# Feature sums, numerators and second pieces of the first fourth-layer batches: from VectorE to GpSimd

## The chip, the cores and the metric

The kernel runs on one core of a Trainium2 chip. The metric is the device time of one execution in microseconds (us); lower is better. A core has five engines with instruction queues of their own: TensorE (PE, with weight loads shown apart as PEld), VectorE (DVE), ScalarE (ACT), GpSimd (POOL) and SyncE (SP), which here only issues DMAs. Each queue runs strictly in its order, and engines wait for each other through semaphores.

## The reference

Four graph layers on x of 8 batches x 2048 nodes x 64 features, with one adjacency matrix of 2048 x 2048 for all batches. After each layer x becomes layernorm(x + layer(x)). The first three layers are attention layers; the fourth weighs each feature by itself:

```python
def _L2_gnn_ref(x, adj, W, a):
    h = jnp.matmul(x, W)
    ...
    e = jax.nn.leaky_relu(f1[:, :, None] + f2[:, None, :], negative_slope=ALPHA)
    e = jnp.where(adj[None, :, :] > 0, e, NEG_BIG)
    attention = jax.nn.softmax(e, axis=2)
    h_prime = jnp.matmul(attention, h)
    return jax.nn.relu(h_prime)

def _L3_gnn_ref(x, w0, b0, wa, ba, adj):
    feat = jax.nn.softplus(x * (INV_SQRT2 * w0[0, 0]) + b0[0])
    scores = feat * wa + ba
    mask = adj > 0
    logits = scores[:, None, :, :] * mask[None, :, :, None].astype(scores.dtype)
    logits = jnp.where(mask[None, :, :, None], logits, jnp.float32(-1000000000.0))
    attn = jax.nn.softmax(logits, axis=2)
    out = jnp.einsum('bijd,bjd->bid', attn, feat)
    return out
```

In the fourth layer the scores depend on the source node and the feature alone. So its softmax is a quotient of two products with the mask: the numerator is mask x (feat * exp(scores)), the denominator is mask x exp(scores). A node without any edge gets the mean of feat over all nodes instead, for which the kernel needs the sum of feat.

## The kernel before

**Units and steps.** Layers 1 to 3 are cut into 24 units, one for each layer and batch. Units 0 to 15 are the first two layers, units 16 to 23 the third layer, so unit 16 + b is batch b's third layer. In the code `now[1]` is the running unit's number. A unit has 16 steps, one for each block of 128 source nodes. In a step of the third layer VectorE makes the weights w of 128 x 2048 out of a row r in PSUM and the mask `edge` in SBUF (`weights`), ScalarE takes their exponential (`exponential`), and PE adds their product to the sums `acc` (`products`). VectorE may run two steps ahead (`reach`), and w has four buffers, so weights of a step wait until PE has used those of four steps before. The row r is one single tile: the next unit's row is spread over it by PE (`spread`) when VectorE has made its last weights of a unit.

**Ends of units.** When a unit's products are done, a generator is put into the background streams (`bg`); each step of the main loop moves every stream on to its next `yield`, which interleaves the unit's end with the steps of the next unit. For the third layer that is first `finish`: copy acc, transpose it on PE (p_o), divide on VectorE (den, o), layernorm. Then comes `l3_features`, which the diff touches. Because the finish takes most of a unit, the softplus of batch b falls at the end of unit 17 + b and what follows it at the start of unit 18 + b. All instructions of PE, VectorE, ScalarE and GpSimd keep the order in which the program emits them; only DMAs are ordered by the framework.

**What `l3_features` does for a batch.** It stores x (tile x_d), computes softplus on ScalarE and one addition on VectorE into f (in place of x, so the profile names it x), then on GpSimd d = f * wa + l3off. The sum of f over a partition's 16 nodes goes to fs, which PE sums over the partitions (p_fm) and VectorE turns into the mean fm (`l3_mean`). ScalarE takes exp(d), VectorE makes the numerator f * d. Then each of the two, f and d, is split into two pieces: ScalarE rounds it [...] (`q.v[0]`), and the rest `q.v[1]` is what a subtraction leaves; four subtractions of 128 x 512 for a batch. Two batches make a pair (i is 0 for the even batch, 1 for the odd one). In the version before, the even batch's subtractions are on GpSimd, the odd one's on VectorE.

**Layer 4's products.** When both batches of a pair are ready, `l3_products` multiplies the pieces with mask blocks (p_l, 32 matmuls for a block of 128 nodes), half a block between two steps of the units from 19 on. Their place in PE's queue is fixed when the program is built. The mask comes in quarters by DMA from a copy in memory (mask_d). `l3_finish` divides on VectorE (nd), adds the mean term, normalizes and stores.

**Group 1.** At the same time, at the turn from unit 17 to unit 18, the generator `group` prepares the constants of the batches 4 to 7: a handful of VectorE operations of 128 x 64 (s_g, tt_g, lo_g, down_g), one exponential on ScalarE (te), then 256 small matmuls (p_lse_g) spread over the steps of unit 18, and again small VectorE operations (am_g, tt_g).

All instructions of the four compute engines are recorded by one helper at line 80, so the profile names them by their tiles.

Of the kernel before, what the change touches and what calls it, by code (L numbers as in the profile page):

```python
# [8 lines left out]
F32 = mybir.dt.float32  # L9
# [6 lines left out]
ALU = mybir.AluOpType  # L16
AX = mybir.AxisListType

P = 128
# [31 lines left out]
def gnn4_kernel(ctx: ExitStack, tc: tile.TileContext, t, out):  # L51
    nc = tc.nc
    x_in, adjT = t["x"], t["adjT"]
    B, N, F = x_in.shape
# [9 lines left out]
    small = ctx.enter_context(tc.tile_pool(name="small", bufs=2))  # L64
# [42 lines left out]
    class Banks:  # L107
# [4 lines left out]
        pool = None  # L112
# [28 lines left out]
    pe, dve, act, pool = (InOrder(e) for e in (nc.tensor, nc.vector, nc.scalar, nc.gpsimd))  # L141

    def psum(name):
        return pm.tile([P, 512], F32, tag="pm", name=name)
# [4 lines left out]
    def bc_k(v, n=K, f=F):  # L149
        return v[:, None, :].to_broadcast([P, n, f])  # L150
# [65 lines left out]
    src = t["L0_gnn_a"]  # L216
# [6 lines left out]
    p = psum("p_nodes")  # L223
# [157 lines left out]
    def softplus(f, y, src, layer=2):  # L381

        act.activation(y, src, AF.Abs, scale=l3c[:, 0:1], bias=l3c[:, 1:2])
        act.activation(y, y, AF.Exp, scale=-1.0)
        yield 1
        act.activation(y, y, AF.Ln, bias=1.0)
        act.activation(f, src, AF.Relu, scale=l3c[:, 0:1], bias=l3c[:, 1:2])
        yield 1 if layer == 2 else 4
        dve.tensor_tensor(f, f, y, ALU.add)
# [785 lines left out]
    now = [0, 0, 0]  # L1175

    def l3_mean(q, i, fs, n):

        yield from pm_slots.take()
        p = psum(f"p_fm_{n}")  # L1180
        pe.matmul(p[:, :F], lhsT=ones, rhs=fs, start=True, stop=True)
        yield 1
        q.fm[i] = small.tile([P, F], F32, tag="fm", name=f"fm_{n}", bufs=4)
        dve.tensor_scalar(q.fm[i], p[:, :F], 1.0 / N, -1.0, ALU.mult, ALU.add)
        pm_slots.give()

    def l3_features(b):

        if b % 2 == 0:
            q = Pair()  # L1190
            q.bs, q.n, q.fm, q.x, q.ready = [b, b + 1], f"{b}", {}, {}, 0
            pairs.append(q)
        else:
            q = pairs[-1]
        i = b % 2
        n = f"3_{b}"
        slots, tag = ((h_slots, "h"), (xT_slots, "xT"))[i]
        yield from slots.take()
        yield from e_slots.take()
        f = x_cur[b].v  # L1200
        q.x[i] = dram.tile([P, K, F], F32, tag="x3_d", name=f"x3_d_{b}", bufs=B)
        nc.sync.dma_start(q.x[i], f)
        y = tmp.tile([P, K, F], F32, tag="e", name=f"sp_{n}")
        yield from softplus(f, y, f)
        e_slots.give()
        d = tmp.tile([P, K, F], F32, tag=tag, name=f"d_{n}")
        pool.tensor_tensor(d, f, bc_k(wa), ALU.mult)
        pool.tensor_tensor(d, d, bc_k(l3off), ALU.add)
        fs = small.tile([P, F], F32, tag="fs", name=f"fs_{n}")
        dve.tensor_reduce(fs, f.rearrange("p k f -> p f k"), AX.X, ALU.add)  # L1210
        bg.add(l3_mean(q, i, fs, n))
        yield 2
        act.activation(d, d, AF.Exp)
        yield 1
        dve.tensor_tensor(f, f, d, ALU.mult)
        yield 1

        if i == 0:
            if b == B - 2:
                while now[0] < 3:  # L1220
                    yield 1
            else:
                yield from v_slots.take()
            q.v = [
                [
                    (work if b == B - 2 else late).tile(
                        [P, K2, 2, 2, F],
                        F32R,
                        tag="w" if b == B - 2 else f"v{m}{h}",
                        name=f"v{m}_{h}_{q.n}",  # L1230
                        bufs=4 if b == B - 2 else 1,
                    )
                    for h in range(2)
                ]
                for m in range(2)
            ]
        else:
            while not hasattr(q, "v"):
                yield 1
        parts = [(h, w, (f, d)[w][:, h * K2 : (h + 1) * K2]) for h in range(2) for w in range(2)]  # L1240
        for h, w, src in parts:
            act.copy(q.v[0][h][:, :, i, w], src)
        yield 1
        eng = dve if i else pool
        for h, w, src in parts:
            eng.tensor_tensor(
                q.v[1][h][:, :, i, w], src, q.v[0][h][:, :, i, w].bitcast(F32), ALU.subtract
            )
        slots.give()
        yield 1  # L1250
        q.ready += 1
# [197 lines left out]
    for n, (layer, b) in enumerate(todo):  # L1449
# [10 lines left out]
        for jb in range(K):  # L1460
# [12 lines left out]
            if jb == K - 1:  # L1473
                end = [lambda u=u: finish(u)]
                if layer < 2:
                    end += [2 if now[0] < 2 else 1, lambda layer=layer, b=b: scores(layer + 1, b)]
                else:
                    end += [1, lambda b=b: l3_features(b)]
                if layer == 1 and b % NB == NB - 1:
                    end += [lambda b=b: group(b // NB)]  # L1480
                bg.add(chain(*end), begun=True)
            elif not done and jb >= 10 and ready(*nxt):
                prepare(*nxt)
                prepared.add(n + 1)
                done = True
# [524 lines left out]
```

## Time and profile before

| what | value |
|---|---|
| median of 3 runs | 1392.18 us (1391.94 to 1396.22) |
| profiled execution, its own time | 1391.82 us |
| its span | 1390.0 us |
| mean granted clock of TensorE | 0.952 |
| VectorE: fs, the sum of f, 128x1024 to 128x64 | 8 instances, 1.907 / 1.960 / 2.016 us (shortest, median, longest) |
| VectorE: numerator, 128x1024 | 3 from 800 to 1000 us: 1.211 / 1.226 / 1.444 us |
| VectorE: second piece, 128x512 | 4 from 840 to 910 us: 0.681 to 0.686 us |
| GpSimd: second piece, 128x512 | 4 from 840 to 910 us: 1.273 to 1.286 us |
| GpSimd: d = f * wa, 128x1024 | 8 instances, median 2.368 us |
| GpSimd: tree of layer 1 (512, then 256, 128, 64 columns) | at 180.35 us: 1.28, then 1.66 for three |

Four places of the span matter. Up to about 912 us only layer 3 runs (the units 16 to 18 and the start of unit 19). At 830 to 840 unit 17 ends and batch 0's features are made; at 884 to 905 unit 18 ends, and batch 1's follow. From 912 on layer 4's products run between the steps. At 951 to 965 unit 19 has ended, and batch 2's features come.

How to read the views: "busy" is the time in which an engine executed something. In a timeline a row gives the start, the length, the engine, the operation with its output and inputs, and in brackets how long the engine stood idle before it and for whom. Several executions of one group that follow each other are one row (x3). In the chain of waits each piece is a start, a length and the group that was under way; it is followed back from the last instruction.

### The profile page before, as it was taken

The page shows a single profiled execution, that of the slowest core. Times are in us where ns is not written, and L with a number is a line of the kernel's source. Part 1 is how long each engine was busy: PE and PEld are TensorE (multiplying, and loading weights), DVE is VectorE, ACT ScalarE, POOL GpSimd, SP SyncE. Part 2 cuts the span into 40 slices and gives each one's busy share as a digit, 9 for nine tenths or more (in the row PEclk, how much of TensorE's full clock was granted, in tenths as well). Part 3 has the DMA queues.
Part 4 walks back from the last instruction along what each step waited for, and adds up shares of the span by engine and source line. Part 5 has one row for each costly group of instructions (what it writes and reads, how often), then busy time and mean ns, then how long its engine had stood idle before and what let it go on. Part 6 is the DMA issues. An engine that isn't in the chain of part 4 may idle for free.

```text
span 1390.0 us, 19341 instructions
## 1 busy us (share of the span) xinstructions
PE 1220.5 (88%) x7169; PEld 623.5 (45%) x7169; DVE 1214.1 (87%) x1108; ACT 751.3 (54%) x1369; POOL 817.7 (59%) x1103
## 2 busy tenths in 40 slices
PE   3689898999898979999997879799989899976996
PEld 3333233333343423343332324255644455666996
DVE  3889889999999999889999899998879798877876
ACT  4444543446245544343436987867666768564432
POOL 1566777558668686756743543343646564676665
PEclk9799999999999999999999989899999899998998
DMA  8640000000000212123101000034443444511111
GB/s 298 227 93 1 1 2 1 1 2 2 1 1 1 91 62 77 62 77 93 32 2 39 1 16 2 21 107 133 138 122 97 123 123 136 162 25 32 35 39 34
DMA packets 112010, 87.24 MB, mean 63 GB/s; under 512 B 57917, under 2 KB 90845, under 8 KB 110882
## 3 DMA queue, kind: packets, MB, share of 16 engines
q1 hardware_dynamic: 111538, 85.79, 20.6%
q8 instruction: 59, 0.97, 0.3%
q14 instruction: 45, 0.37, 0.1%
q10 hardware_dynamic: 368, 0.12, 0.0%
HBM read 60.40 MB, written 25.45 MB: 62 GB/s over the span
## 4 chain that ended last, share of the span: by engine, by line
PE 29%; DVE 15%; ACT 5%; issue 4%; POOL 2%; POOLq 0%; DVEq 0%; ACTq 0%
PE p_l L80 14%; PE acc L80 12%; DVE w L80 8%; DVE o L80 2%; ACT w L80 1%; PE p_o L80 1%; DVE nd L80 1%; DVE x L80 1%; ACT sp L80 1%; DVE fs L80 1%; PE r L80 1%; POOL sq_x L80 1%; POOL st_x L80 0%; PE p_s L80 0%; ACT L80 0%
## 5 line engine op out<-in xcount | busy, mean ns | idle before, releaser
L80 DVE SCALAR_TENSOR_TENSOR w<-r,se,edge 128x2048 f32<-128x2048 f32 (+1 forms) x270 | 552.7, 2101 | 32.2 <-PE r L80 24.5
L80 PE MATMUL acc<-w,pv 128*64 128x512 f32 x2048 | 498.9, 621 | 52.8 <-DVE w L80 41.1
L80 DVE SCALAR_TENSOR_TENSOR w<-r,lo_g,edge 128x2048 f32<-128x2048 f32 (+1 forms) x144 | 297.6, 2097 | 22.1 <-PE acc L80 12.0
L80 ACT ACTIVATE w<-w,down_g 128x2048 f32<-128x2048 f32 (+1 forms) x144 | 257.2, 1810 | 69.2 <-DVE w L80 59.7
L80 PEld LDWEIGHTS p_l<-v,mask 128*128 128x128 f32 x2048 | 256.4, 196 | 61.9 <-issue 47.8
L80 PE MATMUL p_l<-v,mask 128*128 128x256 f32 x2048 | 271.2, 291 | 10.6 <-POOL mask L80 7.0
L80 PEld LDWEIGHTS acc<-w,pv 128*64 128x64 f32 x2048 | 133.0, 139 | 312.4 <-issue 181.0
L80 PE MATMUL acc<-w,x 128*64 128x512 f32 x1024 | 259.1, 637 | 14.5 <-ACT w L80 10.8
L80 POOL TENSOR_TENSOR sq_x<-sq_x 128x32 f32<-128x32 f32 (+4 forms) x207 | 110.0, 532 | 64.8 <-ACT sq_x L80 50.3
L80 PEld LDWEIGHTS acc<-w,x 128*64 128x64 f32 x1024 | 67.0, 142 | 132.0 <-issue 89.2
L80 ACT ACTIVATE o<-p_o,den 128x64 f32<-128x64 f32 x256 | 55.9, 327 | 72.5 <-DVE den L80 72.5
L80 ACT ACTIVATE nd<-p_l,empty 128x256 f32<-128x256 f32 x64 | 30.1, 470 | 109.3 <-PE p_l L80 109.3
L80 PE MATMUL p_o<-rh,oT 128*128 128x130 f32 x384 | 60.1, 293 | 21.1 <-DVE o L80 5.8
L80 PEld LDWEIGHTS p_o<-rh,oT 128*128 128x128 f32 x384 | 49.3, 194 | 54.9 <-issue 34.3
L80 ACT COPY oT<-acc 128x512 f32<-128x512 f32 x48 | 25.6, 585 | 87.9 <-PE acc L80 87.9
L80 POOL TENSOR_TENSOR eh<-eh,x 128x1024 f32<-128x1024 f32 (+2 forms) x24 | 36.4, 1531 | 61.2 <-ACT eh L80 56.7
L80 POOL TENSOR_TENSOR st_x<-isw_x,mhalf 128x16 f32<-128x16 f32 x24 | 70.6, 2940 | 1.9
L80 POOL TENSOR_TENSOR d<-x,wa_bc 128x1024 f32<-128x1024 f32 x8 | 19.0, 2376 | 68.5 <-DVE x L80 68.5
L80 DVE RECIPROCAL nd<-nd 128x256 f32<-128x256 f32 x32 | 55.7, 1742 | 0.0
L80 POOL TENSOR_TENSOR sq_x<-o 128x512 f32<-128x512 f32 x23 | 29.3, 1272 | 41.5 <-DVE o L80 41.3
L80 ACT ACTIVATE xs<-x,nodes 128x64 f32<-128x64 f32 x128 | 44.2, 434 | 3.6 <-PE p_xT L80 3.6
L80 POOL CAST mask<-edge 128x2048 fp32r<-128x2048 fp8e4 x16 | 30.5, 1906 | 24.1 <-PE p_l L80 24.1
(260 smaller groups left out, 1558.4 us busy)
## 6 DMA issues: line engine op xcount, KB each, us to landing
mask<-mask_d SPq DMA_DIRECT2D x132, 256.0 KB
mask_d<-mf SPq DMA_DIRECT2D x32, 512.0 KB
raw<-in_adjT_dram SPq DMA_DIRECT2D x8, 1024.0 KB
raw<-in_adjT_dram SPq DMA_DIRECT2D x16, 512.0 KB
x<-in_x_dram SPq DMA_DIRECT2D x8, 512.0 KB
x_d<-x SPq DMA_DIRECT2D x8, 512.0 KB
e<-x_d SPq DMA_DIRECT2D x64, 64.0 KB
out_dram<-o SPq DMA_DIRECT2D x64, 64.0 KB
```

Source lines behind the costliest of these rows:

```text
L80: ins = f(*args, **kwargs)
```

## The change

For batches whose features are made while the unit's number is below 20, three things go from VectorE to GpSimd. The sum fs becomes a tree of four additions (512, 256, 128 and 64 columns) that uses d's tile as its space, and it stands before the product with wa. The numerator f * d goes to GpSimd, and so do the second pieces of the odd batch. For later batches all stays, except that fs is emitted before d's two operations. The numbers are looked up where each instruction is emitted: batches 0 and 1 get all of it, batch 2 only the tree (its numerator is emitted in unit 20).

```diff
         d = tmp.tile([P, K, F], F32, tag=tag, name=f"d_{n}")
+        fs = small.tile([P, F], F32, tag="fs", name=f"fs_{n}")
+        if now[1] < 20:
+            src = f
+            for m in (8, 4, 2):
+                pool.tensor_tensor(d[:, :m], src[:, :m], src[:, m : 2 * m], ALU.add)
+                src = d
+            pool.tensor_tensor(fs, d[:, 0], d[:, 1], ALU.add)
+        else:
+            dve.tensor_reduce(fs, f.rearrange("p k f -> p f k"), AX.X, ALU.add)
         pool.tensor_tensor(d, f, bc_k(wa), ALU.mult)
         pool.tensor_tensor(d, d, bc_k(l3off), ALU.add)
-        fs = small.tile([P, F], F32, tag="fs", name=f"fs_{n}")
-        dve.tensor_reduce(fs, f.rearrange("p k f -> p f k"), AX.X, ALU.add)
         bg.add(l3_mean(q, i, fs, n))
         yield 2
         act.activation(d, d, AF.Exp)
         yield 1
-        dve.tensor_tensor(f, f, d, ALU.mult)
+        side = pool if now[1] < 20 else dve
+        side.tensor_tensor(f, f, d, ALU.mult)
         yield 1
...
-        eng = dve if i else pool
+        eng = pool if now[1] < 20 or not i else dve
         for h, w, src in parts:
             eng.tensor_tensor(
                 q.v[1][h][:, :, i, w], src, q.v[0][h][:, :, i, w].bitcast(F32), ALU.subtract
             )
```

## The prediction

> **What bounds the kernel now.** I read the page first (busy shares, the 40 slices), then the table of windows around the edited places, then the chain of waits, and last the timeline of each engine there. The page alone settles little: PE 88% and VectorE 87% busy mean that the bound changes from stage to stage. The stages that matter, from the table of windows (columns: length; busy us of PE, PE's weight loads, VectorE, ScalarE, GpSimd; granted clock; DMA):
>
> ```profile
> PE 1220.5 (88%) x7169; PEld 623.5 (45%) x7169; DVE 1214.1 (87%) x1108; ACT 751.3 (54%) x1369; POOL 817.7 (59%) x1103
> ...
> 840.00:880.00 40.00, 35.83 (x345) 15.17 (x344) 38.64 (x34) 31.03 (x24) 19.26 (x28) 0.91 0.01 3
> 880.00:912.00 32.00, 23.91 (x96) 8.20 (x97) 30.30 (x30) 27.93 (x23) 4.75 (x3) 0.84 0.06 22
> 912.00:960.00 48.00, 48.00 (x295) 29.72 (x292) 38.63 (x25) 35.06 (x30) 23.16 (x31) 1.00 0.46 135
> 960.00:1016.00 56.00, 56.00 (x339) 34.22 (x338) 50.46 (x52) 34.59 (x29) 31.50 (x51) 1.00 0.52 149
> ```
>
> The reader sees VectorE full from 840 to 912 (38.64 of 40, 30.30 of 32) and PE full from 912 to 1016, where layer 4's products (p_l) run between layer 3's. So VectorE time saved before 912 can be time, saved after 912 it is none. The chain of waits shows the hand-over:
>
> ```profile
> 894.72 0.96 ACT d L80
> ...
> 896.85 4.61 DVE w L80 x2
> 901.46 2.40 DVE v L80 x4
> ...
> 904.56 1.23 PE p_o L80 x8
> 905.79 7.00 PE acc L80 x24
> 912.79 2.11 PE p_l L80 x16
> ```
>
> Here the four second-piece subtractions (v) of batch 1 are on the path, and PE stands idle in front of p_o until VectorE's division has followed them. Two timelines (start, length, engine, group) show the thing that decides the size:
>
> ```profile
> 834.15 2.36 POOL L80 TENSOR_TENSOR d<-d,l3off 128x1024 f32<-128x1024 f32 x1
> 835.94 0.65 DVE L80 TENSOR_TENSOR s_g<-s,lim_g 128x64 f32<-128x64 f32 x1
> 836.63 0.22 DVE L80 TENSOR_TENSOR tt_g<-s_g,sc_g 128x64 f32<-128x64 f32 x1
> ...
> 865.39 3.35 POOL L80 TENSOR_TENSOR sq_x<-sq_x 128x512 f32<-128x512 f32 x5 [3.85 <-ACT sq_x L80]
> ...
> 865.43 1.32 DVE L80 SCALAR_TENSOR_TENSOR tt_g<-s,sc_g 128x64 f32<-128x64 f32 x1
> 866.79 0.78 DVE L80 TENSOR_TENSOR am_g<-am_g,tt_g 128x64 f32<-128x64 f32 x1
> ```
>
> A 128x64 VectorE operation of 0.22 us takes 0.65, 1.32 or 0.78 us when a GpSimd operation is running, and ends 0.08 us after that one ends (834.15 + 2.36 = 836.51; 835.94 + 0.65 = 836.59).
>
> **What the Trainium skill says.** "SBUF — State Buffer", section "SBUF: two separate sides": VectorE with two SBUF inputs (or in a two-port mode) and GpSimd take one port pair in turns, each for a whole instruction. The lines above agree; the weights w, with one operand in PSUM, run undisturbed (2.34 us beside GpSimd or not). "GPSIMD Engine Reference", section 3.1: tensor_tensor costs GpSimd 1.96 times VectorE's time; here the subtraction takes 1.28 us against 0.684, 1.87 times. "TensorE: Matmul & The Clock Gate", Part 1: after a quiet window of about 3.4 us PE runs at half clock for about as long. Here far shorter gaps did it: idle 846.14 to 847.07, then clock 0.55, 0.50, 0.50 in the three microseconds from 848 and eight products in 3.32 us, not 1.94. Yet a gap of 0.67 us at 893.6 did nothing, so I can't forecast single dips.
>
> **The change part by part.** The order of instructions is unchanged on PE and ScalarE; VectorE loses nine, GpSimd gains eighteen, two DMAs swap places with neighbours on SP's queue. Durations are of the profiled execution, 1391.82 us with a span of 1390.0, 0.36 below the median of 1392.18.
>
> Removed from VectorE: three sums fs of 1.99 (batches 0, 1, 2), two numerators of 1.22 (batches 0, 1; batch 2's comes when the unit's number is already 20 and stays), four subtractions of 0.684 (batch 1; those of batch 0 are on GpSimd already): 5.97 + 2.44 + 2.74 = 11.1 us. Added to GpSimd: three trees, each 1.28 + 0.08 + 1.66 = 3.02 as a tree of the same four shapes at 180.35 takes, two numerators of 2.4, four subtractions in 4.95: 9.1 + 4.8 + 5.0 = 18.9 us. It idles 7 to 21 us in a stretch around these places, so its busy time costs nothing in itself.
>
> *End of unit 17 (batch 0), 831 to 884.* VectorE's next weights start 1.98 earlier, at 831.6, and end at 834.05. But GpSimd now runs without a break: tree 831.70 to 834.70, d's product to 837.15, d's addition to 839.60 (before: to 836.51). Into that fall group 1's small VectorE operations: s_g, tt_g, a second tt_g after ScalarE's te, lo_g, each with two SBUF inputs. s_g waits for the tree's third step (834.38), the first tt_g for its fourth (834.78), the second tt_g for d's product (837.23), lo_g for d's addition (839.68). The weights of unit 18's step 1 then start at 840.05, not 838.25: 1.8 late in place of 1.9 early. Queued behind: the division that frees p_o's bank and all later weights. Step 1's product starts about 844.35, not 843.31; VectorE then regains 1.22, because the numerator is gone, and 0.54 where it waited for p_o at 852.52. It is level at about 856 (+0.1), or about 1.2 late if the longer PE gap (1.15 us at 843.2) brings a half-clock stretch beside or in place of the one at 848. From 867 VectorE paces, so this carries over: I take +0.6. Bounds: without the port conflict -0.9 (PE's own row of p_lse and p_o work holds it there) or -2.1 (if the dip at 848 goes too); with two dips +2.5. Tree in time: fs at 834.70, p_fm on PE at 836.14. d is ready at 839.60, ScalarE takes it at 840.16 anyway, and GpSimd's numerator is done at 843.7, ahead of the cast at 845.05.
>
> *End of unit 18 (batch 1), 884 to 912.* After the softplus VectorE has only operations with a PSUM operand, so no conflict. Its weights start at 886.1 instead of 888.02, then wait for w's buffers (PE's steps 13 to 15 end 889.2, 891.05, 893.3); without fs, numerator and subtractions the first division comes at 898.5, not 903.78. PE ends step 2 at 901.45 and goes on with p_o at once: its idle 3.11 us go. Late next is ScalarE: its casts still end at 901.42, its exponentials of steps 3, 4, 5 at 903.4, 905.3, 907.2; PE's third product ends at 909.1, where p_l started at 912.79: -3.7. A half-clock stretch as before at 906.4 leaves -2.2. I take -3.0. GpSimd: tree to 889.1, d at 894.05 (ScalarE takes it at 894.61), numerator at 898.0 (the cast is at 899.35; 1.3 us of cover, beyond which each microsecond is one on ScalarE's in-order queue), second pieces 900.0 to 905.0, before p_l needs them at 909.
>
> *End of unit 19 (batch 2), 951.* PE is full here, so the 1.98 saved are worth nothing. GpSimd's d comes 3.0 later (960.2; ScalarE takes it at 960.26), and its power for the first output block delays VectorE at 960.94 by about 1, so the weights of step 3 reach PE up to 0.4 late: +0.2. On SP's queue x's store (waits for VectorE's x at 931.4) now stands before one mask load, which leaves about 1 us later; it is used some 8 us after its issue: nothing.
>
> Sum: +0.6 - 3.0 + 0.2 = -2.2, kept through the full PE stretch to 1016 and the unchanged rest: 1391.82 - 2.2 = 1389.6.
>
> **The rivals.** *Full gain:* the port conflict misses (tt_g and lo_g slip between GpSimd's operations). For it: gaps of 0.08 us lie between those. Against it: am_g lost just that race at 866.79. Then -0.9 or -2.1 with -3.7 or -2.2: around -4.6, 1387.2; at best 1386.0. *Slower:* the same conflict at 835 to 840, with half-clock stretches after both of PE's new gaps (843 and 847), costs +2.5 by 867, and the dip after 902 leaves only -2.2; with +0.4 at batch 2 and one further chance dip of 1.5 in the boundaries after 1016, +2.2: 1394.0. It decides once unit 18 starts its step 10 over 2.2 us late. Against it: PE had a dip there before as well, so only the second is new. *No effect:* p_l starts no earlier, because something else holds PE (ScalarE's casts late behind GpSimd's numerator, using up the 1.3 us): about 1392.
>
> **How the numbers follow.** Partial gain 0.52 (1389.6), full gain 0.24, slower 0.15, no effect 0.09. What can be told from no change is about 0.3%, 4.2 us. Only the full gain reaches beyond it, in most of its cases (0.18), with a few of the partial one (0.05): faster 0.23. Of the slower case, two thirds could exceed it if dips add up in later stages as well: 0.10. Within: 0.67. The range reaches from the best full gain to the slower case: 1386.0 to 1394.0.
>
> **What would show it.** Right: p_l's first product near 910, no wait before p_o near 902, and near 837 to 840 two 128x64 VectorE operations of about 2 us each, weights of unit 18's step 1 near 840. Wrong: these operations at 0.22 us (then the full gain), or ScalarE waiting for GpSimd's x ahead of the casts, or p_l waiting for v. The three fs groups on VectorE must fall from eight instances to five, 128x1024 numerators from eight to six.

## The result, and the profile after

The changed kernel takes 1387.09 us (median of 22 runs, 1382.32 to 1390.02) against 1390.61 us (22 runs, 1384.20 to 1396.22) for the one before: a ratio of 0.9970 with a 95% interval of 0.9959 to 0.9982. Run once more later, beside runs of before in the same series, it gave 0.9979 (0.9964 to 0.9993), so the gain is about 0.3%, some 3 us.

The first part of the page of the changed kernel, the busy time of each engine:

```profile
PE 1209.8 (88%) x7169; PEld 620.8 (45%) x7169; DVE 1208.8 (88%) x1099; ACT 751.0 (54%) x1369; POOL 835.9 (61%) x1121
```

And its table of windows (columns as in the prediction's):

```profile
840.00:880.00 40.00, 33.86 (x341) 14.29 (x338) 39.02 (x33) 30.45 (x23) 21.64 (x29) 0.96 0.01 3
880.00:912.00 32.00, 26.47 (x120) 10.00 (x121) 30.14 (x26) 30.49 (x25) 18.19 (x17) 0.89 0.09 29
912.00:960.00 48.00, 48.00 (x290) 28.63 (x286) 35.29 (x26) 35.09 (x31) 23.62 (x31) 1.00 0.45 136
960.00:1016.00 56.00, 56.00 (x347) 35.23 (x346) 48.13 (x48) 34.05 (x30) 31.43 (x49) 1.00 0.53 154
```

GpSimd has 18.2 us more work and VectorE 5.3 less. (11.1 were moved off VectorE; its busy time includes what it stands waiting for the port: two of its small operations alone took 4.3 us more.) From 880 to 912 GpSimd went from 4.75 to 18.19 us and ScalarE from 27.93 to 30.49 of 32: ScalarE is as full there now as VectorE (30.14). Beyond 912 PE is full as before. The chain of waits in that stretch:

```profile
894.08 1.07 ACT d L80
895.15 3.78 ACT w L80 x2
898.93 2.07 ACT v L80 x4
901.00 1.91 ACT w L80
...
902.95 5.72 PE acc L80 x24
908.68 2.10 PE p_l L80 x16
```

Where VectorE's w, v and den stood, ScalarE's casts v and exponentials w stand now, and p_o is gone from the chain. In PE's timeline p_o no longer waits for VectorE; the wait that is left, 0.94 us, is for ScalarE:

```profile
897.09 3.83 PE L80 MATMUL acc<-w,x 128*64 128x512 f32 x16 [0.30 <-ACT w L80]
900.85 1.16 PE L80 MATMUL p_o<-rh,oT 128*128 128x130 f32 x8
902.95 5.72 PE L80 MATMUL acc<-w,x 128*64 128x512 f32 x24 [0.94 <-ACT w L80]
908.61 2.17 PE L80 MATMUL p_l<-v,mask 128*128 128x256 f32 x16
```

At the end of unit 17, the timelines of GpSimd and VectorE in the changed kernel show the cost:

```profile
830.98 1.28 POOL L80 TENSOR_TENSOR d<-x 128x512 f32<-128x512 f32 x1 [11.35 <-DVE x L80]
832.34 1.27 POOL L80 TENSOR_TENSOR d<-d 128x256 f32<-128x256 f32 x2
833.68 0.32 POOL L80 TENSOR_TENSOR fs<-d 128x64 f32<-128x64 f32 x1
834.08 2.37 POOL L80 TENSOR_TENSOR d<-x,wa_bc 128x1024 f32<-128x1024 f32 x1
836.53 2.35 POOL L80 TENSOR_TENSOR d<-d,l3off 128x1024 f32<-128x1024 f32 x1
...
834.11 2.40 DVE L80 TENSOR_SCALAR lo_g<-s_g 128x64 f32<-128x64 f32 x1
836.42 0.21 DVE L80 SCALAR_TENSOR_TENSOR tt_g<-s_g,sc_g 128x64 f32<-128x64 f32 x1
836.67 2.29 DVE L80 TENSOR_TENSOR lo_g<-lo_g,tt_g 128x64 f32<-128x64 f32 x1
...
839.38 2.34 DVE L80 SCALAR_TENSOR_TENSOR w<-r,lo_g,edge 128x2048 f32<-128x2048 f32 x1
```

Two VectorE operations of 0.2 us take 2.40 and 2.29 us. Each ends 0.06 to 0.08 us after a GpSimd operation does (834.08 + 2.37 = 836.45, 836.53 + 2.35 = 838.88), and the weights of unit 18's step 1 start at 839.38.

The span of this profiled execution, 1380.9 us, is 9.1 below that of before; the medians differ by 3.5. To see what the change did, I use times between two marks of one trace. A is from PE's spread of the row at the end of unit 17 to that at the end of unit 18; B from there to the first p_l; C is the last part of B, from the first p_o of unit 18's end to the first p_l. A + B is 83.77 us before and 80.38 after: -3.4. The start up to the first mark (828.95 and 828.23) and the rest after the first p_l (1390.0 - 912.72 = 477.3 and 1380.9 - 908.61 = 472.3) make up the other 5.7. Chance is enough for that, as e2 below shows: only batch 0's part is moved there, and in both of these parts each engine executes what it did before, in the same order. Yet its first mark comes at 834.86, 5.9 us later than before, and its rest is 470.9, 6.4 shorter.

### The profile page after: what moved, and what is told of

Read it like the earlier page. It is cut to its first block, busy times and chain, and to the rows that moved or that the text cites. A ratio compares the mean times of both kernels' runs of the same rounds, so it can differ in the third digit from the quotient of the medians.

```text
span 1380.9 us, 19353 instructions
## 1 busy us (share of the span) xinstructions
PE 1209.8 (88%) x7169; PEld 620.8 (45%) x7169; DVE 1208.8 (88%) x1099; ACT 751.0 (54%) x1369; POOL 835.9 (61%) x1121
## 4 chain that ended last, share of the span: by engine, by line
PE 28%; DVE 15%; ACT 6%; issue 4%; POOL 2%; DMA 0%; POOLq 0%; DVEq 0%; ACTq 0%
PE p_l L80 14%; PE acc L80 11%; DVE w L80 8%; ACT w L80 2%; DVE o L80 2%; DVE nd L80 1%; DVE x L80 1%; ACT sp L80 1%; PE p_o L80 1%; PE r L80 1%; DVE fs L80 1%; ACT v L80 1%; POOL sq_x L80 1%; POOL st_x L80 1%; PE p_s L80 0%
## 5 line engine op out<-in xcount | busy, mean ns | idle before, releaser
L80 PE MATMUL p_l<-v,mask 128*128 128x256 f32 x2048 | 270.7, 291 | 11.1 <-POOL mask L80 6.2
L80 PE MATMUL acc<-w,x 128*64 128x512 f32 x1024 | 253.1, 623 | 16.7 <-ACT w L80 13.3
L80 POOL TENSOR_TENSOR st_h<-isw_h,mhalf 128x16 f32<-128x16 f32 x8 | 24.0, 2994 | 36.6 <-DVE isw_h L80 25.2
L80 POOL TENSOR_SCALAR isw<-isw 128x4 f32<-128x4 f32 x32 | 9.2, 287 | 55.5 <-DVE isw L80 44.3
```

The source lines that it names most:

```text
L80: ins = f(*args, **kwargs)
```

## The experiments

Each row is one profiled execution. "Rest" is from the first p_l to the end of the span.

| kernel | A | B | C | A + B | rest |
|---|---|---|---|---|---|
| before | 55.05 | 28.72 | 16.56 | 83.77 | 477.3 |
| changed | 55.37 | 25.01 | 12.98 | 80.38 | 472.3 |
| changed, second profile (e10) | 55.55 | 24.86 | 12.98 | 80.41 | 470.9 |
| e1, no tree for batch 0 | 52.77 | 26.25 | 12.98 | 79.02 | 471.9 |
| e2, batch 0 alone | 54.47 | 30.72 | 17.63 | 85.19 | 470.9 |
| e3, batch 1's pieces back | 54.68 | 26.86 | 13.71 | 81.54 | 472.5 |
| e4, numerators alone | 52.79 | 26.98 | 13.72 | 79.77 | 474.6 |
| e5, the same program as e4 | 52.86 | 26.14 | 13.72 | 79.00 | 471.0 |
| e6, e1 with trees up to unit 22 | 52.61 | 26.35 | 12.98 | 78.96 | 468.4 |
| e7, changed with the limit at unit 23 | 55.55 | 26.54 | 12.98 | 82.09 | 468.8 |
| e8, the same program as e6 | 52.80 | 26.01 | 12.98 | 78.81 | 470.0 |
| e9, e6 with numerators up to unit 22 | 52.77 | 26.26 | 12.97 | 79.03 | 468.3 |

C repeats to 0.01 us between profiles of the same program, A to 0.2 in the three programs that were profiled twice. But up to the second mark the changed kernel, e10, e7, e2 and e3 execute the same instructions, and their A runs from 54.47 to 55.55: a half-clock stretch follows PE's gap near the new weights in the first three (A 55.37 to 55.55) and not in e2 and e3 (54.47 and 54.68). The six profiles without batch 0's tree have 52.61 to 52.86.

B less its C part goes by the half-clock stretch around the second mark, the spread at the end of unit 18: 11.88 to 12.42 us in the four profiles in which that lasted 6.8 us (before, changed, e10, e5), 13.03 to 13.56 in the eight in which it lasted 10.2. So the reading goes by A and C.

**e1: batch 0's sum stays on VectorE.**

```diff
-        if now[1] < 20:
+        if b > 0 and now[1] < 20:
             src = f
```

> Batch 0's sum stays on VectorE; all else as in the changed kernel. A is the time from PE's spread of the row at the end of unit 17 to that at the end of unit 18 (before 828.95 to 884.00 = 55.05, after 55.37), B from there to the first p_l (before 28.72, after 25.01). Port theory: GpSimd's stream at 831 to 839 is short again, no 128x64 VectorE operation takes over 1 us there, the weights of unit 18's step 1 come some 9.3 us after the spread as before (after: 11.15), and the numerator's 1.22 us and the idle time at p_o are gained: A 54.1, or 53.0 if PE has no half-clock stretch near 848; B 25.0. Time 1 to 2 us below the changed kernel. Rival (VectorE's sum of work sets A, every microsecond moved counts): VectorE has 1.98 more than after, A 57.

1384.02 us (20 runs), ratio to before 0.9959 (0.9944 to 0.9974): 3.1 below the changed kernel's median, or 1.5 by the ratios, whose intervals overlap. So the proof is in the trace. VectorE's timeline at the end of unit 17:

```profile
835.55 0.67 DVE L80 TENSOR_TENSOR s_g<-s,lim_g 128x64 f32<-128x64 f32 x1
...
836.98 0.22 DVE L80 SCALAR_TENSOR_TENSOR tt_g<-s_g,sc_g 128x64 f32<-128x64 f32 x1 [0.30 <-ACT te L80]
837.24 0.23 DVE L80 TENSOR_TENSOR lo_g<-lo_g,tt_g 128x64 f32<-128x64 f32 x1
...
837.88 2.35 DVE L80 SCALAR_TENSOR_TENSOR w<-r,lo_g,edge 128x2048 f32<-128x2048 f32 x1
```

VectorE does 1.99 us more there, and yet its weights start 9.32 us after the spread (837.88 - 828.56), not 11.15 (839.38 - 828.23). A is 52.77, 2.6 below the changed kernel, where the rival had 57: for batch 0 the tree costs more than it saves. Some 1.8 of the 2.6 are the waits and what follows from them (54.47 and 54.68 in e2 and e3), the rest the half-clock stretch. PE's granted clock is 1.00 in all windows from 844 to 856, so the half-clock stretch that before had at 848 and the changed kernel at 844 is gone, as the lower of the two expected values of A takes for granted. B was expected at 25.0 and is 26.25; C, 12.98, is that of the changed kernel to 0.01, so the difference lies in front of p_o, where half clock lasted 10.2 us here and 6.8 in the changed kernel.

**e2: batch 0 alone.** Tree, numerator and subtractions with `b == 0` for the limit.

> Only batch 0's tree and numerator are on GpSimd, batches 1 and 2 as before the change. Theory (all the gain is made at the end of unit 18, by batch 1): A 55.4, B 28.7, no gain. Rival (each batch's share of the moved VectorE work counts): batch 0 has 3.2 of the 11.1 us, so A about 52 to 53.

1392.73 us (one run). A is 54.47, between the two expectations and nearer to the first; the port's waits are there (tt_g 2.01, lo_g 2.39 us), and PE kept its clock. The 0.6 below before is no gain of the 3.2 us taken from VectorE: the changed kernel executes the same up to here and has 55.37 and 55.55, and the A of before has a half-clock stretch in it. The share that the rival counts, 2 to 3 us, is out either way. At the end of unit 18 it is the kernel before, and so is the chain of waits:

```profile
907.73 2.40 DVE v L80 x4
...
910.83 2.07 PE p_o L80 x8
912.90 7.22 PE acc L80 x24
```

C is 17.63, and with p_o in 2.07 us instead of 1.23 the half-clock stretch is worse than in the profile of before (16.56): it lasts 6.8 us, not 3.4. No gain is made here without batch 1's part.

**e3: batch 1's four subtractions back on VectorE.**

```diff
-        eng = pool if now[1] < 20 or not i else dve
+        eng = pool if False or not i else dve
```

> As the changed kernel, but batch 1's four subtractions are back on VectorE (2.74 us). Theory: ScalarE's exponentials behind its casts set PE's steps 3 to 5, so VectorE has slack of about 2.5 us before p_o; the division comes 2.7 later, PE waits about 1 us at p_o, and B is 25.0 to 25.5 (26.5 if that wait brings a half-clock stretch). Rival (additive, the v row stood on the chain of waits with 2.40 us): B 27.4 to 27.7.

1386.48 us (one run). PE's timeline:

```profile
898.46 1.16 PE L80 MATMUL p_o<-rh,oT 128*128 128x130 f32 x8
905.50 1.23 PE L80 MATMUL p_o<-rh,oT 128*128 128x130 f32 x8 [1.75 <-DVE den L80]
912.17 2.18 PE L80 MATMUL p_l<-v,mask 128*128 128x256 f32 x16
```

PE waits 1.75 us at p_o, not the 1 us that was expected, and only 0.73 us of that are left in C (13.71 against 12.98): 0.94 us of PE's wait for ScalarE, which the changed kernel had behind p_o, fall together with it. Of the row that stood on the chain with 2.40 us, taking it away is worth 0.73. (B itself, 26.86, lies above what was expected for the same reason as e1's.)

**e4 and e5: the numerators alone.** The trees' limit and the subtractions' limit are set to False.

> Only the numerators of batches 0 and 1 are on GpSimd; sums and subtractions as before the change. Theory: at the first boundary as without the tree of batch 0, A 54.1 or 53.0; at the second the division comes 1.2 earlier than before, PE's wait at p_o is 2.0 of the 3.1, B 26.5, or 28 with the half-clock stretch after it. Rival (additive): A 53.8, B 27.5.

> The numerators of batches 0 and 1 alone, timed (the kernel of e4). Theory: it has e1's gain in unit 18 (no conflict at the port, A 52.8) and loses 0.7 us of the gain between p_o and p_l: about 0.7 us above e1, 1 to 2 us below the changed kernel, so a ratio of 0.996 to 0.997 to before. Rival (additive, 2.44 of 11.1 us): ratio 0.9993.

e4: 1385.46 us (one run). e5: 1384.66 us (14 runs), ratio 0.9971 (0.9959 to 0.9983), just above what was expected; that it is below the changed kernel (0.9970 and 0.9979) is not shown. A is 52.79 and 52.86, C twice 13.72. PE's wait at p_o is 1.74 us instead of 3.11, and no half-clock stretch follows it. (With 2.0 expected and a stretch as the worse case, B was forecast at 26.5 or 28; it is 26.98 and 26.14.) So 2.44 of the 11.1 us moved bring all that any run gained in A, and 2.8 of the 3.6 us that C lost. Additive shares are refuted: they gave a ratio of 0.9993.

**e6 and e8: trees without batch 0, but up to unit 22.**

```diff
-        if now[1] < 20:
+        if 0 < b and now[1] < 23:
             src = f
```

> As e1, but the trees also for the batches 3 to 5 or 6 (all whose sum is emitted before unit 23). Theory: at the ends of units 20 to 22 the sum (1.94 us) stands on the chain of waits between softplus and the next weights, so each end gains up to 1.9; d comes 3.0 later, at batch 3 ScalarE takes it 4.9 us after it was ready, so that is hidden: 2 to 5 us below e1. Rival (PE is the bound there, and GpSimd's tree only holds up the normalization's small VectorE operations at the port): 0 to 3 us above e1.

> The kernel of e6 again, beside the changed kernel in the same call. If e6's gain is real (no tree for batch 0, trees up to unit 22): ratio to before 0.993 to 0.996, and below the changed kernel by more than the two intervals overlap. If e6 drew lucky half-clock stretches: as e1, 0.996.

1380.29 us (6 runs), ratio 0.9942 (0.9913 to 0.9970); again 1381.40 us (8 runs), 0.9938 (0.9917 to 0.9959). In the chain of waits of before, a sum stands after the softplus at the ends of units 20 to 22; in e6 ScalarE's work follows at once at the end of unit 20 and the division at the end of 21, and at the end of 22 the chain is PE's products. Before, then e6, at the end of unit 21:

```profile
1100.70 1.24 DVE x L80
1101.96 1.93 DVE fs L80
...
1104.01 0.43 DVE o L80
```

```profile
1091.79 1.23 DVE x L80
1093.01 0.10 DVE den L80
1093.14 0.42 DVE o L80
```

From the row's spread at the end of unit 20 to that at the end of unit 22 it is 135.44 us in e6 and 135.28 in e8, against 136.89 in both profiles of the changed kernel and 137.19 in e1: 1.5 to 1.9 less. The medians differ from e1's by 3.7 and 2.6; the intervals of e1 and e6 overlap, so how much of that is real is open. e8 was timed beside the changed kernel (e10, 0.9979, 0.9964 to 0.9993), and there the intervals do not overlap: it is faster than that, by some 6 us.

**e7: the changed kernel with the limit at unit 23 for all three parts.**

> The changed kernel with its limit at unit 23 in place of 20: tree, numerator and second pieces on GpSimd for nearly all batches. Theory: the sum's gain as in e6, but the numerator costs 1.2 us and the odd batch's pieces 2.3 us of latency more, on a GpSimd that also normalizes the outputs; the pair is ready later, and where p_l waits for it that is lost: between 3 us below and 3 us above the changed kernel. Rival (VectorE's work is what counts): 5 us or more below it.

1386.29 us (20 runs), ratio 0.9976 (0.9964 to 0.9989): no better than the changed kernel, as far as this can tell, though VectorE has 8.7 us less to do (1200.1 against 1208.8). The rival's 5 us are out. Batch 0's conflict is back (A 55.55), and of GpSimd's eight subtractions in a row seven come on the chain:

```profile
1057.38 9.65 POOL v L80 x7
```

Yet from unit 20's spread to unit 22's it is 135.74 us here, 0.3 above e6, so in this execution the subtractions cost next to nothing. Batch 0's part explains 3 us of the 5 to 6 between the medians of e7 and those of e6 and e8; the other part stays open.

**e9: e6 with the numerators up to unit 22 as well.**

> As e6, and the numerators up to unit 22 on GpSimd too; second pieces as in the changed kernel. Theory: e7 lost in the odd batch's subtractions on GpSimd (9.65 us on its chain of waits), not in the numerators: within 1.5 us of e6. If the numerators' longer latency costs as well: as e7, 3 to 5 us above e6.

1378.03 us (6 runs), ratio 0.9921 (0.9892 to 0.9950). No cost of the numerators shows there. That they bring something beyond e6 is not shown either: the median is 2.3 us lower, but the intervals overlap, and A + B and the rest are e6's. It has the lowest median of the study, 0.8% below the kernel before.

**e10: the changed kernel again.**

> The changed kernel once more: ratio to before 0.996 to 0.998. The time from the first p_l to the end varies by several microseconds between executions of one program, from half-clock stretches: here 471 to 478 us (first profile after: 472.3, before: 477.3).

1387.34 us (22 runs), ratio 0.9979 (0.9964 to 0.9993). VectorE's timeline:

```profile
836.57 2.02 DVE L80 SCALAR_TENSOR_TENSOR tt_g<-s_g,sc_g 128x64 f32<-128x64 f32 x1 [0.30 <-ACT te L80]
838.62 2.39 DVE L80 TENSOR_TENSOR lo_g<-lo_g,tt_g 128x64 f32<-128x64 f32 x1
```

Here the port's waits fell on the second tt_g and on lo_g's addition, exactly the two that the prediction named, where in the first profile lo_g's tensor_scalar took the first one. e2, e3 and e7 have it as here. The weights start 11.22 us after the spread, beside 11.15, and A is 55.55. The rest after the first p_l, 470.9 us, is just below what was expected.

## Why the prediction was right

It forecast -2.2 us, and the medians say -3.5 (-5.7 to -2.5 by the interval). The signs that it named came: the two long waits, the weights near 840 (839.38), no wait for VectorE at p_o, p_l's first product at 908.61, and on VectorE five sums in place of eight and six numerators in place of eight. The three terms:

*End of unit 17, +0.6 expected.* A grew by 0.32 and 0.50. The mechanism is shown: the weights of step 1 were forecast for 11.1 us after the spread (840.05 - 828.95) and came at 11.15 to 11.24 in all five profiles with batch 0's tree; e1, with VectorE doing more and GpSimd less in the same stretch, has them 1.8 us earlier and A 2.6 shorter. The clock stretch that the longer gap was to bring "beside or in place of the one at 848" came in its place (clock 0.51, 0.50, 0.50 from 844 on). In e2 and e3 it did not come, and their A is 0.58 and 0.37 below that of before, which has a stretch of its own. So both of the prediction's cases occurred, level and late by a clock stretch, each 0.5 to 0.9 us lower than forecast, and against before the sign of this term depends on where the stretch falls. One detail was wrong: the second tt_g was named as the first to wait for a whole operation, and a tensor_scalar with one input was taken as free. Either can be it.

*End of unit 18, -3.0 expected, between -3.7 and -2.2.* The mis-sized term. B fell by 3.71 and 3.86 (half clock at the second mark lasted 6.8 us in all three profiles), and C alone by 3.58: the full value without a half-clock stretch behind p_o, which was taken at half weight. Every profile in which p_o waited under 2 us was without one, and both with a wait of 3.11 had it. That ScalarE is late next is what the chain says, and it agrees with e3, where 2.74 us put back cost 0.73; no run made ScalarE itself faster.

*End of unit 19, +0.2 expected.* From the first p_l to the row's spread at the end of unit 19 it is 29.88 us before and 29.86 after, and from there to unit 20's 64.87 and 64.88: nothing. ScalarE took d at 956.21, about as late relative to p_l (47.6 us) as before (47.54), and VectorE's wait of 1.86 us for GpSimd's power fell into its slack. x's store ahead of a mask load cost nothing either.

The rivals: full gain needed the conflict to miss, and it did not; the slower case needed two half-clock stretches at the first end and one at the second, and there was one and none; no effect needed something else in front of p_l, and ScalarE, the candidate, held PE for 0.94 us only.

The number itself had some luck. 1389.6 was counted from one execution, 1391.82, which lies 1.2 us above the median of 22 runs. The measured 1387.09 is 1.1 us inside the range and stands at the time given for the full gain (1387.2), which needed the conflict to miss. The time alone would have named the wrong case; the traces name the one that was forecast.

What the prediction did not have is how much less would have done: the numerators alone have about the time of all three parts together (0.9971 beside 0.9970), as batch 0's tree gives back more (2.6 in A, e1) than the tree and the pieces of batch 1 add (0.7 in C). By these marks they would even be 1.9 us faster, which the intervals neither show nor exclude.

## What to carry to other kernels

Work that is taken off a full engine is worth its length only until the next engine is late: here the first 1.2 us at a boundary brought 2.8 (with the clock stretch that had followed the wait), the next 4.7 only 0.7. Before moving work to GpSimd, look for what VectorE executes meanwhile: operations that read and write SBUF alone can wait out GpSimd's whole instruction, however short they are (0.2 us became 2.0 to 2.4 here). And compare marks within one trace: over the whole span, chance moved single executions more than the change did.

## What the runs showed of the hardware

A VectorE tensor_scalar of 128x64 floats, one SBUF input, was held by a GpSimd operation as well: 2.40 us where it takes 0.185 elsewhere, in one of the profiles. The prediction had counted only operations with two inputs. TensorE's clock went to half after gaps of 0.93 us (before, at 846), 1.19 us (changed, at 843) and 3.11 us (before and e2, at p_o), for 3.4 us each time but 6.8 in e2, and not after gaps of 0.94 us (changed, at 902), 0.96 us (e2, at 849.5) and 1.75 us (e3, at p_o).

The length of a gap alone doesn't decide it; where it falls matters as well. In all twelve traces the half-clock stretches begin on a fixed grid of 3.41 us, which lies differently in each execution, and up to the last microseconds of a trace they last whole cells of it. PE's idle time, counted in each full-clock cell from 100 to 1370 us, tells what follows. Of the 123 cells with 2.1 us or more, all were followed by half clock; of the 4009 with less than 1.8 us, 32 were; between them 24 of 42. This explains a pair of equal gaps of 2.13 us, PE waiting for ScalarE's w near 870: in before the whole gap lies in one cell (868.58 to 871.99), and half clock follows (three products in 7.05 us from 871.98); in the changed kernel the grid cuts it into 1.87 and 0.26 us at 871.33, and the clock stays (1.94 us each from 871.58). The gaps of 0.93 and 1.19 us are among the 32, and why these brought half clock stays open.

Two profiles of one program differ by up to 3.6 us in the rest after the first p_l (e4 and e5: 474.6 and 471.0). Half clock after 905 us adds up to 42.4 us in e4 and 36.3 in e5, and 6.1 us at half clock are about 3 us of PE's work.
